# A transformer block with four-bit feed-forward weights: the last down pass staggered over four tiles, x rows in eight places, lookups queued behind the copies

## The chip, the cores and the metric

The kernel runs on one core of a Trainium2 chip. The metric is the device time of one execution in microseconds (us); lower is better. Kernels are compared by the median of several executions, and one execution of each is recorded by the hardware profiler. In a profile PE is TensorE (matmuls), PEld its weight loads, DVE VectorE, ACT ScalarE, POOL GpSimd, and SP the engine whose queue issues all DMAs here.

## The reference, cut to what matters

```python
x = x + layernorm(attention(layernorm(x)) @ Wo)          # 2048 rows of 1024
h = layernorm(x)
Wg, Wu, Wd = (NF4[codes] * scale_of_64 for each matrix)  # 2752 x 1024, 2752 x 1024, 1024 x 2752
inter = silu(h @ Wg.T) * (h @ Wu.T)                      # 2048 x 2752
x = x + layernorm(inter @ Wd.T)                          # 2048 x 1024
```

The attention is causal, with 16 heads of 64 and rotary positions. Each feed-forward weight is a code from 0 to 15, looked up in a table of 16 values and multiplied by a scale that is shared by 64 inputs. The change touches only the last line: the product with `Wd`, its layer norm and the residual sum.

## The kernel before

Matrix products are made with three matmuls: each operand is split into a high part and the rest, and high x high, high x rest and rest x high are summed in PSUM (`mm3`, lines 112 to 117). The split is one ACT copy and one DVE subtraction (`split`, L120 and L121).

The stages follow each other: layer norm and the q, k, v projections, attention, output projection with residual (up to about 1710 us in the profile), gate and up products with their lookups (to about 2640), and then the down product (to the end).

**The down product.** `inter` lies in DRAM as 22 tiles for each half of the rows, `ind[g][kt]`. The output is made in four passes, for column half `n` and row half `g` in the order (0,0), (0,1), (1,0), (1,1). A pass uses all eight PSUM banks, one for each of its eight row tiles of 128 rows; for each `kt` an `it` tile of 1 MB is loaded (L613, the last one in two halves by L616) and multiplied into all eight banks with the weights `wd[n, kt]`. At the end of each of the first three passes eight ACT copies (`keep`, L632) bring the banks into SBUF, so that the next pass can have the banks. Since the layer norm goes over a whole row, a row tile is complete when both column halves are there: `finish` is called for row tiles 0 to 7 after the pass (1,0), and for 8 to 15 in the pass (1,1), the last one, where the right half is read from its bank directly.

**The lookups.** `down_weights` makes the weights of one `kt` from the codes by `looked_up`: three loads of codes and scales (`cs`, L489 to L491), then seven ACT lines (L498) and ten DVE operations, which together stand for the table as a sum of minima and maxima of straight lines, and the split. `make` says how far the lookups are to be by each step: in the first pass one ahead of PE, in the second pass up to 16 of the second column half, and the last six with `issue_after` behind the second pass's copies on ACT. These are not orders of issue but program order: a scheduler fixes each engine's instruction order when the program is built, by program order and by its own estimate of when each operand and slot is ready. [...]

**Slots in SBUF.** Tiles with one tag share a fixed number of slots, and a new tile waits until a slot of its tag is given up. Seven `hd` slots hold the `it` tiles and the kept sums of the left column half (two while the second pass runs, four while the third does, two in the last pass once row tiles 0 to 7 are finished). `cs` tiles have the three `pw` slots, the lookups' results `mp` the four `f4` slots, the x rows that `finish` loads the two `pb` slots, and the results `y` go to `f4` slots.

**The last pass.** The tiles with `kt >= NIT - LAST`, that is the last six, are held: PE is to use them bank by bank, so that the first bank is complete early and its `finish` can run beside the matmuls of the others. With two `hd` slots taken by sums, five are left for six held tiles. The scheduler resolved this in its own way: the built order has five held tiles used for all eight banks, and then the sixth for all eight.

**`finish`** (L634 to L643) for one row tile: load the x row tile, BNStats over both halves (L126), mean and variance (L128, L130), the power -1/2 on POOL (L132), the bias (L134), and for each half an ACT addition of the bias (L641), a DVE multiply-add into `y` (L642) and a store (L643).

Of the kernel before, what the change touches and what calls it, by code (L numbers as in the profile page):

```python
# [10 lines left out]
F32 = mybir.dt.float32  # L11
# [4 lines left out]
ALU = mybir.AluOpType  # L16
# [5 lines left out]
E = 1024  # L22
D = 64
I = 2752
P = 128
# [3 lines left out]
NIT = 22  # L29
# [28 lines left out]
def block_kernel(ctx, tc, x, wq, wk, wv, wo, gu_codes, gu_scales, d_codes, d_scales, cos_sin, out):  # L58
    nc = tc.nc
    V, A, G, T = nc.vector, nc.scalar, nc.gpsimd, nc.tensor  # L60
    load = nc.sync.dma_start
# [12 lines left out]
    def slot(tag, shape, dtype, name):  # L74
        assert int(np.prod(shape[1:])) * 4 <= SLOTS[tag][1] * 1024, (tag, shape)
        return sb.tile(shape, dtype, tag=tag, name=name, bufs=SLOTS[tag][0])
# [6 lines left out]
    def any_bank():  # L83
        turn[0] += 1
        return bank(BANK_ORDER[turn[0] % 8])
# [37 lines left out]
    def ln_stats(row):  # L123
        st = small.tile([P, 2, 6], F32, tag="st", name="st")
        for i in range(2):
            V.bn_stats(st[:, i, :], row[i])  # L126
        mv = small.tile([P, 2], F32, tag="mv", name="mv")
        V.bn_aggr(mv, st.rearrange("p a b -> p (a b)"))  # L128
        ve = small.tile([P, 1], F32, tag="ve", name="ve")
        V.tensor_scalar(ve, mv[:, 1:2], EPS, None, ALU.add)  # L130
        rs = small.tile([P, 1], F32, tag="rs", name="rs")
        G.tensor_tensor(rs, ve, nhalf, ALU.pow)  # L132
        nb = small.tile([P, 1], F32, tag="nb", name="nb")
        V.tensor_scalar(nb, mv[:, 0:1], rs, -1.0, ALU.mult, ALU.mult)  # L134
        return mv[:, 0:1], rs, nb
# [449 lines left out]
        ["pa"] * 4 + ["w"] * 3 + ["pa"] + ["xc"] * 3,  # L585
        ["pa", "xc"] + ["pa"] * 4 + ["w"] * 3 + ["pa", "xc"],
    )
    LAST = 6
    SECOND = 16
    wd = {}  # L590

    def down_weights(n, kt):

        ns = slice(n * 512, (n + 1) * 512)
        if kt % 2 == 0:
            t = slot(WD_TAGS[n][kt // 2], [P, 2, 2, 512], FR, "wd")
            wd[n, kt], wd[n, kt + 1] = t[:, :, 0], t[:, :, 1]
        t = wd[n, kt]
        rows = P if kt < NIT - 1 else D
        b1 = min(2 * kt + 1, 42)  # L600
        m = looked_up(
            d_codes[kt * P : kt * P + rows, ns], d_scales[2 * kt : 2 * kt + 1, ns], d_scales[b1 : b1 + 1, ns], rows
        )
        if rows == P:
            split(t[:, 0], t[:, 1], m)
        else:
            A.copy(t[:, 0], m)
            V.tensor_tensor(t[D:, 0], m[D:], f32(t[D:, 0]), ALU.subtract)

    def load_inter(g, kt):  # L610
        t = slot("hd", [P, 2, 2, 512], FR, "it")
        if kt < NIT - 1:
            load(f32(t), ind[g][kt])  # L613
        else:
            for a in range(2):
                load(f32(t[a * D : (a + 1) * D]), ind[g][kt][:D])  # L616
        return t

    def down(o, it_, w, tt, first, last):

        i = it_[:, tt // 4, :, tt % 4 * P : (tt % 4 + 1) * P]
        if not last:
            mm3(o, i, w, first, False)
        else:
            T.matmul(o, lhsT=i[:, 0], rhs=w[:, 0], start=False, stop=False)
            T.matmul(o, lhsT=i[:, 1], rhs=w[:, 0], start=False, stop=True)

    def keep(t, o, n):

        if t % 4 == 0:  # L630
            kept.setdefault(n, []).append(slot(("hd", "xc")[n], [P, 4, 512], F32, "kept"))
        return A.copy(kept[n][t // 4][:, t % 4], o)  # L632

    def finish(t, left, right):  # L634

        xt = slot("pb", [P, E], F32, "xt")
        load(xt, x1d[t * P : (t + 1) * P, :])
        y = slot("f4", [P, E], F32, "y")
        _, rs, nb = ln_stats((left, right))
        for src, h in ((right, slice(512, E)), (left, slice(0, 512))):  # L640
            A.activation(xt[:, h], xt[:, h], AF.Identity, bias=nb)  # L641
            V.scalar_tensor_tensor(y[:, h], src, rs, xt[:, h], ALU.mult, ALU.add)  # L642
            load(out[t * P : (t + 1) * P, h], y[:, h])  # L643

    kept = {}
    left = [(n, kt) for n in range(2) for kt in range(NIT)]

    def make(upto):
        while left and 2 * NIT - len(left) < upto:
            down_weights(*left.pop(0))  # L650

    for n in range(2):
        for g in range(2):
            os = [any_bank() for _ in range(8)]
            final = n == 1 and g == 1
            its = []
            for kt in range(NIT):

                make(kt + 1 if (n, g) == (0, 0) else NIT + min(4 + kt, SECOND) if (n, g) == (0, 1) else 2 * NIT)
                it_ = load_inter(g, kt)  # L660
                if final and kt >= NIT - LAST:
                    its.append(it_)
                    continue
                for tt in range(8):
                    down(os[tt], it_, wd[n, kt], tt, kt == 0, kt == NIT - 1)
            for tt in range(8):
                t = 8 * g + tt
                for i, it_ in enumerate(its):
                    kt = NIT - LAST + i
                    down(os[tt], it_, wd[n, kt], tt, False, kt == NIT - 1)  # L670
                if final:
                    finish(t, kept[0][t // 4][:, t % 4], os[tt])
                else:
                    last = keep(t, os[tt], n)
            if (n, g) == (0, 1):
                with tc.issue_after(last.ins):
                    make(2 * NIT)
            if (n, g) == (1, 0):
                for t in range(8):
                    finish(t, *(kept[i][t // 4][:, t % 4] for i in range(2)))  # L680
# [49 lines left out]
```

## Time and profile before

| | us |
|---|---|
| Median of 3 runs | 3162.13 (3154.66 to 3164.9) |
| The profiled execution | 3162.79 |
| Its span | 3161.0 |
| PE busy | 3007.8, 95% of the span |
| DVE, ACT, POOL busy | 2161.6, 1827.9, 700.3 |
| First down pass, last matmul starts | 2758.37 |
| Second pass, first matmul starts | 2765.32 |
| Third pass, first matmul starts | 2885.67 |
| Last pass, first matmul starts | 3003.54 |
| Last matmul starts | 3127.32 |
| Granted TensorE clock, mean | 0.977 |

The span is the time from the first to the last instruction in the profile; the execution's own time is a little longer. A line of the timeline gives the start, the length of an instruction (of the merged group, where there are several), its engine, its line in the program, the operation with the tile that it writes and the tiles that it reads, and in brackets the idle time of its engine ahead of it with what is thought to have ended it. For SPq the length is only that of issuing; the transfer lands later. Matmul ends are modelled: a matmul of 128 x 512 is shown with 0.39 us, while in a full stream one starts each 0.227 us.

### The profile page before, as it was taken

How to read it: one execution, taken by the hardware profiler on the slowest of the kernel's cores; microseconds unless marked ns; L12 is line 12 of the kernel's file. 1: busy time of each engine (PE TensorE's matmuls, PEld its weight loads, DVE VectorE, ACT ScalarE, POOL GpSimd, SP SyncE). 2: the span in 40 equal slices, each digit the busy share in tenths (PEclk: the TensorE clock that was granted, in tenths of full speed). 3: DMA queues.
4: the chain of work that ended last, by engine and by line, in shares of the span. 5: the costliest groups of instructions: out<-in, count | busy, mean ns of one | idle time of the engine just before them, and what ended most of it. 6: DMA issues, size and time to landing. Idle time of an engine off the chain costs nothing.

```text
span 3161.0 us, 43388 instructions
## 1 busy us (share of the span) xinstructions
PE 3007.8 (95%) x14656; PEld 2474.5 (78%) x14656; DVE 2161.6 (68%) x4428; ACT 1827.9 (58%) x3846; POOL 700.3 (22%) x888
## 2 busy tenths in 40 slices
PE   7979999999999999989889999999999999999995
PEld 6868887787877777877667888888888888788884
DVE  7457778777877777776565986677666688974022
ACT  3246667666766666666555865556555567864011
POOL 4334444444443334453221000000000000000000
PEclk9989999999999999999989999999999999999997
DMA  8777666566637675643355332232222338685584
GB/s 311 251 233 228 206 207 198 169 187 189 201 133 198 194 223 158 218 141 111 113 193 167 120 114 94 100 106 95 94 93 94 107 101 289 212 283 193 193 328 145
DMA packets 246495, 552.31 MB, mean 175 GB/s; under 512 B 20224, under 2 KB 110336, under 8 KB 219136
## 3 DMA queue, kind: packets, MB, share of 16 engines
q1 hardware_dynamic: 246272, 549.53, 53.3%
q8 instruction: 116, 1.90, 0.2%
q14 instruction: 107, 0.88, 0.1%
HBM read 403.70 MB, written 145.75 MB: 174 GB/s over the span
## 4 chain that ended last, share of the span: by engine, by line
PE 79%; DMA 9%; DVE 6%; ACT 2%; issue 1%; SPq 1%; POOL 1%; DVEq 0%; ACTq 0%; POOLq 0%
PE bk L114 13%; PE bk L115 13%; PE bk L116 13%; PE pt L294 6%; PE qkv L114 5%; PE qkv L116 5%; PE qkv L115 5%; PE o L299 3%; PE s L255 3%; PE o L298 3%; PE s L257 3%; DMA wf<-in_wq 1%; DMA xc<-xd 1%; DMA cs<-in_d_codes 1%; PE pj L440 1%
## 5 line engine op out<-in xcount | busy, mean ns | idle before, releaser
L498 ACT ACTIVATE ln<-cs,bias 128x512 f32<-128x512 f32 x910 | 610.7, 717 | 133.6 <-DVE mp L505 37.1
L114 PE MATMUL bk<-x,wt 128*128 128x512 f32 x1376 | 535.8, 390 | 0.0
L115 PE MATMUL bk<-x,wt 128*128 128x512 f32 x1376 | 535.4, 389 | 0.0
L116 PE MATMUL bk<-x,wt 128*128 128x512 f32 x1376 | 535.2, 389 | 0.0
L284 POOL TENSOR_SCALAR prob<-prob,rc 128x512 f32<-128x512 f32 (+3 forms) x640 | 405.3, 654 | 407.8 <-DVE rc L279 241.1
L262 ACT ACTIVATE prob<-s,mxs 128x512 f32<-128x512 f32 (+3 forms) x640 | 400.8, 629 | 158.4 <-DVE mxs L261 144.0
L121 DVE TENSOR_TENSOR pw<-pt,pw 128x512 fp32r<-128x512 f32 (+3 forms) x640 | 376.8, 601 | 130.8 <-ACT pw L120 128.9
L261 DVE TENSOR_REDUCE mxs<-s 128x1 f32<-128x512 f32 (+3 forms) x640 | 379.5, 601 | 99.4 <-PE s L257 60.0
L120 ACT CAST pw<-pt 128x512 fp32r<-128x512 f32 (+3 forms) x640 | 323.1, 525 | 165.5 <-PE pt L294 135.1
L132 POOL TENSOR_TENSOR rs<-ve,nhalf 128x1 f32<-128x1 f32 x64 | 40.3, 643 | 1578.9 <-DVE ve L130 1553.8
L294 PE MATMUL pt<-ident,prob 128*128 128x128 f32 x2176 | 346.4, 276 | 3.2 <-DVE pw L121 3.0
L294 PEld LDWEIGHTS pt<-ident,prob 128*128 128x128 f32 x2176 | 267.5, 142 | 57.2 <-issue 4.4
L255 PE MATMUL s<-k,q 128*128 128x512 f32 (+3 forms) x640 | 268.1, 419 | 35.2 <-ACT prob L262 33.5
L114 PEld LDWEIGHTS bk<-x,wt 128*128 128x128 f32 x1376 | 258.8, 188 | 53.7
L115 PEld LDWEIGHTS bk<-x,wt 128*128 128x128 f32 x1376 | 258.6, 188 | 53.7
L116 PEld LDWEIGHTS bk<-x,wt 128*128 128x128 f32 x1376 | 258.5, 188 | 53.5
L114 PE MATMUL bk<-wd,it 128*128 128x512 f32 x672 | 262.6, 391 | 6.6 <-ACT kept L632 6.6
L115 PE MATMUL bk<-wd,it 128*128 128x512 f32 x672 | 262.4, 390 | 0.0
L116 PE MATMUL bk<-wd,it 128*128 128x512 f32 x672 | 261.8, 390 | 0.0
L299 PE MATMUL o<-pw,v 128*128 128x512 f32 (+3 forms) x640 | 250.9, 394 | 4.9 <-DVE pw L121 4.4
L298 PE MATMUL o<-pw,v 128*128 128x512 f32 (+3 forms) x640 | 247.7, 388 | 5.5 <-ACT pw L120 4.7
L114 PE MATMUL qkv<-xc,w 128*128 128x512 f32 x576 | 234.7, 407 | 14.5 <-ACT w L173 8.5
(124 smaller groups left out, 5516.3 us busy)
## 6 DMA issues: line engine op xcount, KB each, us to landing
xc<-xd SPq DMA_DIRECT2D x96, 1024.0 KB, 9.0
it<-ind SPq DMA_DIRECT2D x84, 1024.0 KB, 6.2
ind<-hl SPq DMA_DIRECT2D x84, 512.0 KB, 2.6
q<-qs SPq DMA_DIRECT2D x128, 256.0 KB, 6.9
cs<-in_gu_scales SPq DMA_DIRECT2D x172, 128.0 KB, 3.1
cs<-in_gu_codes SPq DMA_DIRECT2D x86, 256.0 KB, 2.9
tab<-in_cos_sin SPq DMA_DIRECT2D x32, 512.0 KB, 9.8
xd<-xr SPq DMA_DIRECT2D x16, 1024.0 KB, 6.6
```

The lines of the kernel that those rows point to most:

```text
L114: r = T.matmul(o, lhsT=w[:, 0], rhs=xx[:, 0], start=first, stop=False)
L115: T.matmul(o, lhsT=w[:, 0], rhs=xx[:, 1], start=False, stop=False)
L116: T.matmul(o, lhsT=w[:, 1], rhs=xx[:, 0], start=False, stop=last)
L121: V.tensor_tensor(lo, src, f32(hi), ALU.subtract)
L255: mm = T.matmul(s, lhsT=q[:, 0, j * P : (j + 1) * P], rhs=k[:, b:e], start=True, stop=False)
L261: V.tensor_reduce(mx, s, AX.X, ALU.max, negate=True)
L262: A.activation(prob[i][:, j, : e - b], s, AF.Exp, bias=mx, accum_out=sums[:, j % BATCH, i : i + 1])
L284: G.tensor_scalar(p, p, rc[:, jj % BATCH, i : i + 1], 0.0, ALU.mult, ALU.add)
L294: T.transpose(pt[:, j * P : (j + 1) * P], prob[kb // 4][:, j, kb % 4 * P : (kb % 4 + 1) * P], ident)
L298: T.matmul(o[:, cs], lhsT=v[:, kb, :], rhs=pw[:, 0, cs], start=kb == 0, stop=False)
L299: T.matmul(o[:, cs], lhsT=v[:, kb, :], rhs=pw[:, 1, cs], start=False, stop=kb == nk - 1)
L498: A.activation(ln, c8, AF.Identity, bias=bias_of[ab], scale=ab[0])
```

## The change

Three things change. The number of held tiles in the last pass, `LAST`, goes from six to four. `finish` loads its x row tile into one of eight slots by the number of its row tile (four `f4`, two `pb`, two `pw`) in place of the two `pb` slots, and writes its result over it, so that the tile `y` is gone. And in the second pass the lookups for the second column half are traced with `issue_after` behind the last copy of the first pass, which holds their ACT instructions behind that copy in ACT's order; the call that asked for everything in the later passes is dropped, since everything is asked for by then.

```diff
-    LAST = 6
+    LAST = 4
     SECOND = 16
+    XT_TAGS = ["f4"] * 4 + ["pb"] * 2 + ["pw"] * 2
     wd = {}
...
     def finish(t, left, right):
 
-        xt = slot("pb", [P, E], F32, "xt")
+        xt = slot(XT_TAGS[t % 8], [P, E], F32, "xt")
         load(xt, x1d[t * P : (t + 1) * P, :])
-        y = slot("f4", [P, E], F32, "y")
         _, rs, nb = ln_stats((left, right))
         for src, h in ((right, slice(512, E)), (left, slice(0, 512))):
             A.activation(xt[:, h], xt[:, h], AF.Identity, bias=nb)
-            V.scalar_tensor_tensor(y[:, h], src, rs, xt[:, h], ALU.mult, ALU.add)
-            load(out[t * P : (t + 1) * P, h], y[:, h])
+            V.scalar_tensor_tensor(xt[:, h], src, rs, xt[:, h], ALU.mult, ALU.add)
+            load(out[t * P : (t + 1) * P, h], xt[:, h])
 
     kept = {}
+    last = None
...
             for kt in range(NIT):
-
-                make(kt + 1 if (n, g) == (0, 0) else NIT + min(4 + kt, SECOND) if (n, g) == (0, 1) else 2 * NIT)
+                if (n, g) == (0, 0):
+                    make(kt + 1)
+                elif (n, g) == (0, 1):
+
+                    with tc.issue_after(last.ins):
+                        make(NIT + min(4 + kt, SECOND))
                 it_ = load_inter(g, kt)
```

## The prediction

> **What bounds the kernel now.** I read the page's busy shares first (PE 95%, so whatever shortens the run must take out PE idle time or the time after the last matmul), then the idle time of PE by stage, then the timeline around each gap. All that the change touches lies after 2640 us: the four down passes. The table by stage (columns: length, then busy us and instructions of PE, PEld, DVE, ACT, POOL, granted clock, DMA share, GB/s):
>
> ```profile
> 2640.00:2759.00 119.00, 118.75 (x524) 98.02 (x523) 109.82 (x197) 93.19 (x143) 0.00 (x0) 1.00 0.74 241
> 2759.00:2765.00 6.00, 0.00 (x0) 0.00 (x0) 6.00 (x11) 6.00 (x12) 0.00 (x0) 0.89 0.90 352
> 2765.00:2885.00 120.00, 119.69 (x518) 98.95 (x519) 62.78 (x109) 52.38 (x84) 0.00 (x0) 0.98 0.71 237
> 2885.00:3004.00 119.00, 119.00 (x527) 98.57 (x526) 39.75 (x72) 36.64 (x60) 0.00 (x1) 1.00 0.62 212
> 3004.00:3116.00 112.00, 112.00 (x495) 92.64 (x494) 20.12 (x49) 11.28 (x18) 4.75 (x8) 1.00 0.67 254
> 3116.00:3122.00 6.00, 2.03 (x9) 1.34 (x8) 0.00 (x0) 0.00 (x0) 0.00 (x0) 1.00 0.75 175
> 3122.00:3128.00 6.00, 5.34 (x16) 3.98 (x16) 4.20 (x11) 0.00 (x0) 0.55 (x1) 0.72 0.00 0
> 3128.00:3161.00 33.00, 0.00 (x0) 0.00 (x0) 16.69 (x43) 10.67 (x16) 3.83 (x7) 0.56 0.67 223
> ```
>
> See three holes in PE and nothing else: 2759 to 2765, 3118 to 3122, and the 33 us after the last matmul. The timeline at the first hole:
>
> ```profile
> 2757.49 0.59 SPq L491 DMA_DIRECT2D cs<-in_d_scales  x1
> 2758.20 3.31 SPq L613 DMA_DIRECT2D it<-ind  x5
> 2758.37 0.39 PE L626 MATMUL bk<-wd,it 128*128 128x512 f32 x1
> ...
> 2760.58 1.04 ACT L632 COPY kept<-bk 128x512 f32<-128x512 f32 x2
> ...
> 2765.32 0.77 PE L114 MATMUL bk<-wd,it 128*128 128x512 f32 x1 [6.56 <-ACT kept L632]
> ```
>
> The releaser named is ACT, but the first copy was done at about 2761.1. The first `it` load of the pass was issued at 2758.20, behind the lookups' `cs` loads in SP's queue; the DMA view puts loads of that moment at 7.0 us or more to landing, that is 2765.2. So two things made the hole: copies behind lookups on ACT, and, ending later, `it` loads behind `cs` loads on SP. The second hole, and the end:
>
> ```profile
> 3115.34 1.09 SPq L616 DMA_DIRECT2D it<-ind  x2
> 3122.37 0.77 PE L625 MATMUL bk<-wd,it 128*128 128x512 f32 x1 [4.34 <-DMA it<-ind]
> ...
> 3146.43 0.99 SPq L643 DMA_DIRECT2D out<-y  x2
> 3147.53 0.37 SPq L637 DMA_DIRECT2D xt<-x1d  x1
> 3148.73 1.33 ACT L641 ACTIVATE xt<-xt,nb 128x512 f32<-128x512 f32 x2 [2.49 <-DMA xt<-x1d]
> ...
> 3151.36 0.40 SPq L637 DMA_DIRECT2D xt<-x1d  x1
> 3152.34 1.33 ACT L641 ACTIVATE xt<-xt,nb 128x512 f32<-128x512 f32 x2 [2.28 <-DMA xt<-x1d]
> ```
>
> The sixth held tile has no `hd` slot until a held one is given up, so its load starts at 3115.34, and all eight banks end together at 3127.5. Then eight `finish` calls run with two `pb` slots for x rows: load, ACT, DVE, some 3.7 us a row, one after another.
>
> **What the Trainium skill says.** "TensorE: Matmul & The Clock Gate", the part on the HAM clock gate: an idle window of about 3.4 us throws PE to half clock, and it takes about as much sustained work to come back. The trace agrees: after 2765.32 and after 3122.37 the first dozen or so matmuls start 0.43 us apart instead of 0.227. So a hole costs more than its length. "DMA: Bandwidth & Descriptors", anatomy of one DMA: a semaphore wait is served on the issuing sequencer before dispatch. So on SP a waiting load holds all behind it, which the first hole shows. The same page, on bandwidth, names 435 GB/s as the ceiling on the fabric side; the trace runs at 425 GB/s with a DMA share of 1.03 in 3030 to 3040, so I take 430 as full.
>
> **The change, part by part.** Sums are against the profiled execution (span 3161.0, time 3162.79, that is 1.8 outside the span; 0.7 above the median of 3162.13). A pass is 22 x 8 x 3 - 8 = 520 matmuls x 0.2267 = 117.9 us (2885.67 to 3003.54 confirms it).
>
> 1. Lookups behind the first pass's copies. In the built order ACT now has the eight copies straight behind the last first-half lookup, and SP has the six first `it` loads of the second pass ahead of the `cs` load of lookup 3. Lookup 21's codes were read by 2724, so these loads leave as soon as PE frees slots, over 10 us before they are wanted. ACT is idle by then; the copies (0.5 us a bank) run as at 2882.70, where PE didn't wait. Removed: 2765.32 - 2758.60 = 6.7 us of hole, and the slow clock behind it: the second pass took 2885.67 - 2765.32 = 120.4 instead of 117.9, 2.5 us. Sum 9.2.
>  What it costs: the head start. Before, four lookups and most of a fifth of the second half were made in the first pass (ACT casts at 2731, 2738, 2744, 2750), and sixteen were done by 2837. Now they start at about 2760. The pace where nothing blocked is 6.3 us (2737.7, 2744.0, 2750.3); sixteen end at about 2861. The second pass's copies, which stand behind them on ACT, are due from 2873, the weights from 2876. Margin 12 us, hence 0. At the first pass's pace with loads in the way (eleven lookups from 2648.5 to 2724.2, 6.9 each) they end at 2870: still 0. On SP `it` 20 and 21 stand behind `cs` 15 (about 2842, wanted after 2867); the third pass's first `it` behind `cs` 18 (2861 to 2865, lands about 5 to 7 later, wanted at 2876). Bounds: 0 to +5. Lookups 16 to 21 stand behind the second pass's copies in both kernels.
>
> 2. x rows into eight places (`f4` x4, `pb` x2, `pw` x2), result over the row. No instruction is added: 16 loads, 32 ACT, 32 DVE, 32 stores as before. What moves is when loads go. Six x rows now stand among the third pass's `it` loads on SP, and the three in `pw` wait for the last lookups' `cs` slots (about 2914, 2920 and 2924 in the old times). Behind these stand `it` 7, 8, 9, which go at 2914.5, 2920.5, 2925; wanted at 2885.7 + 5.44k = 2923.8, 2929.2, 2934.7. With the least landing of 4.7 us, plus 1.2 for each half megabyte ahead, they land at 2920.4, 2926.4, 2931. Margin 3 us; I take 0, bounds 0 to +6 in all.
>  In the last pass the first eight `finish` calls, whose sixteen stores stand among the `it` loads on SP, end at about 21 us into the pass (DVE, 8 x (4 x 0.64 + 0.5) = 24 from 3001) instead of 44. DMA has 8.5 MB in this stretch, 20 us at 430 GB/s; `it` 7 then lands about 31 in, wanted at 38. Hidden; the cover is five `hd` slots of prefetch.
>
> 3. Four held tiles. Two `hd` slots hold the left sums, five are left: four held and the one before. They fit, so banks end one by one: 11 matmuls, 2.5 us apart. `it` 21 takes the slot that `it` 16 gives up 92.5 into the pass; with the 7.0 us that it took before it lands at 99.6. The built order puts 15 matmuls ahead of its first use: 98 + 3.4 = 101.4. So the second hole goes: 3122.37 - 3117.87 = 4.5, and 16 matmuls in 5.2 instead of 3.6: sum 6.1. Margin 1.8, bounds 0 to +4 with the clock.
>
> 4. The end. Before: 3161.0 - 3127.5 = 33.5 us after the last matmul. Now all x rows are in SBUF long before, and DVE works at 2.4 to 3.0 us a tile against PE's 2.5, so at the last matmul only two tiles or so are left. By the DVE order, from PE's end: BNStats of the last bank to 0.7; the product of tile 13 and small ones to 2.6; `pow` on POOL and `nb` back at 3.7; ACT of tiles 14 and 15 to 5.5 (each 0.7); last two products to 6.5; store 2.0 to 2.8 (min and median of the stores at the end). I take 9.3. Lower bound 7 (one tile alone), upper 14 (DVE a further tile and a half late). Removed: 24.2, bounds 19 to 26.
>
> Sum: 9.2 + 6.1 + 24.2 = 39.5. Span 3121.5, this execution 3123.3, on the median 3122.6: **3123**.
>
> **Rivals.**
> A. The transfers come late: x rows and `it` loads meet in the third pass, or the stores and loads at the start of the last. For it: margins of 2 to 7 us, and in 3020 to 3060 DMA is full. Against: PE didn't stall there with DMA at 1.03. Two or three waits of 3 to 5 us and a clock dip: 3127 to 3140, say 3133.
> B. DVE becomes the bound of the staggered end: its instructions wait in order for PE, POOL and ACT, so each tile costs 3.7 us as now. 8 x (3.7 - 2.5) = 9.6 later: 3133.
> C. The stagger doesn't come about (the last `it` is late again). Then only the x rows and the first hole help: tail of 8 x 3 = 24 instead of 33.5, and 9.2: 3144.
> D. Slower. With the head start gone, the second pass's copies on ACT stand behind sixteen lookups, and PE can't begin the third pass without banks. Late by 16p - 113 us at p us a lookup; this eats 39.5 from p = 9.5, and at p = 10 the time is 3172 or so with the clock. The worst seen is 6.9. For it: each `cs` load is now behind an `it` load that waits for PE. Against: PE frees a slot each 5.44 us, faster than lookups eat.
>
> **How the numbers follow.** Forecast 0.72, A 0.11, B 0.07, C 0.05, D 0.03, and 0.02 that gains and losses cancel. The forecast's own range: 3161.0 + 1.8 - (9.2 + 6.1 + 26) = 3121.5 at best, 3143 with all upper bounds at once (5 + 6 + 4 + 4.7), 3133 with half of them. The runs of before spread from 3154.7 to 3164.9, so I widen downwards by 7. To leave no more than 2 in 10 out: 3114 to 3136. What this kernel's measurement can tell from no change is 0.3%, 9.5 us: faster 0.94, same 0.02, slower 0.04.
>
> **What would show it.** PE without a gap over 1 us from 2640 to about 3112 and 1.00 clock throughout; the copies of the first pass at about 2755.5, without activations in between; last ACT cast of the sixteen before 2873; `it` 21 issued about 9 us before its first use; products spread over the last 20 us of PE, and 9 us from the last matmul to the end. A gap at the start of the third pass would be D, one in the middle of it or about 20 to 40 us into the last pass A, and over 14 us after the last matmul B. It would be wrong, too, if PE's clock fell where now it is 1.00.

## The result

| | before | changed |
|---|---|---|
| Median, us (4 runs each) | 3163.52 (3154.66 to 3175.01) | 3127.32 (3123.55 to 3129.2) |
| Ratio, 95% interval | | 0.9882 (0.9849 to 0.9916) |
| Span of the profiled execution | 3161.0 | 3125.7 |
| PE busy | 3007.8, 95% | 3003.9, 96% |
| Granted clock, mean | 0.977 | 0.982 |

The span is 35.3 us shorter. That number holds something that is not the change's work: up to the last matmul of the first down pass both programs do the same on PE, yet that matmul starts at 2761.06 us instead of 2758.37, 2.7 later. So from here on I measure from that matmul to the end of the span and call this stretch T. It was 3161.0 - 2758.37 = 402.6 before and 3125.7 - 2761.06 = 364.6 after: a gain of 38.0 us, where the prediction's sum was 39.5.

The profile after, by stage (the columns are those of the table of before):

```profile
2759.00:2765.00 6.00, 6.00 (x28) 4.96 (x27) 4.34 (x8) 6.00 (x12) 0.00 (x0) 1.00 0.83 291
2765.00:2879.00 114.00, 114.00 (x505) 94.33 (x503) 98.14 (x173) 84.34 (x130) 0.00 (x0) 1.00 0.75 244
2879.00:2885.00 6.00, 5.42 (x25) 4.26 (x24) 3.95 (x7) 5.74 (x11) 0.00 (x0) 1.00 0.78 314
2885.00:3100.00 215.00, 214.41 (x946) 177.11 (x945) 55.22 (x113) 41.62 (x65) 4.77 (x8) 1.00 0.73 262
3100.00:3117.00 17.00, 16.83 (x75) 13.60 (x73) 15.78 (x41) 7.81 (x12) 3.30 (x6) 1.00 0.36 134
3117.00:3126.00 9.00, 0.00 (x0) 0.00 (x0) 5.04 (x12) 2.79 (x5) 1.10 (x2) 0.74 0.58 216
```

PE's busy time equals the length of the stage in the first two rows. In the third and fourth 0.6 us each is missing, and the clock is 1.00 until the last matmul. The three holes of before are now two cracks and 9 us at the end. DVE, idle for most of the last pass before, works 15.78 of the 17 us ahead of PE's end.

The timeline at the first pass's end, where 6.7 us had been lost (the changed kernel has the `it` loads at L614 and L617 and the copies at L633):

```profile
2757.86 3.95 SPq L614 DMA_DIRECT2D it<-ind  x2
2758.32 4.01 ACT L633 COPY kept<-bk 128x512 f32<-128x512 f32 x8 [31.16 <-PE bk L627]
2761.06 0.39 PE L627 MATMUL bk<-wd,it 128*128 128x512 f32 x1
2761.29 0.39 PE L114 MATMUL bk<-wd,it 128*128 128x512 f32 x1
```

All eight copies are one block with no activation in between, ACT had waited 31 us for the banks, and PE goes from pass to pass in 0.23 us, its normal step. At the second pass's end:

```profile
2871.90 0.62 ACT L120 CAST wd<-mp 128x512 fp32r<-128x512 f32 x1 [3.05 <-DVE mp L511]
2871.93 0.33 SPq L489 DMA_DIRECT2D cs<-in_d_codes  x1
2873.51 6.16 SPq L614 DMA_DIRECT2D it<-ind  x3
2876.18 4.01 ACT L633 COPY kept<-bk 128x512 f32<-128x512 f32 x8 [3.66 <-PE bk L627]
2879.90 0.47 PE L114 MATMUL bk<-wd,it 128*128 128x512 f32 x1 [0.58 <-DMA it<-ind]
```

The sixteenth lookup's cast is done 3.7 us before the copies can start. But the DVE operation that releases this cast (L511) is also the one that gives up the `cs` slot for which SP's queue waits, and the third pass's first `it` load stands behind those `cs` loads: it goes at 2873.51 and PE gets it at 2879.90, 0.74 us after its normal step. And the end:

```profile
3116.44 0.39 PE L627 MATMUL bk<-wd,it 128*128 128x512 f32 x1
3116.87 0.70 DVE L126 BATCH_NORM_STATS2 st<-bk 128x6 f32<-128x512 f32 x1 [0.23 <-PE bk L627]
3119.17 2.56 ACT L641 ACTIVATE xt<-xt,nb 128x512 f32<-128x512 f32 x4 [1.94 <-DVE nb L134]
3122.03 0.74 DVE L642 SCALAR_TENSOR_TENSOR xt<-kept,rs,xt 128x512 f32<-128x512 f32 x1
```

The last product ends at 3122.77, 6.1 us after PE (which ends at 3116.44 + 0.23), and the last store 2.9 later.

### The profile page after: what moved, and what is told of

It reads as the page before. It is cut to its first block, busy times and chain, and to the rows that moved or that the text cites. A ratio compares the mean times of both kernels' runs of the same rounds, so it can differ in the third digit from the quotient of the medians.

```text
span 3125.7 us, 43392 instructions
## 1 busy us (share of the span) xinstructions
PE 3003.9 (96%) x14656; PEld 2470.5 (79%) x14656; DVE 2161.1 (69%) x4428; ACT 1831.5 (59%) x3846; POOL 702.8 (22%) x888
## 4 chain that ended last, share of the span: by engine, by line
PE 42%; DMA 3%; DVE 3%; ACT 1%; issue 1%; SPq 0%; DVEq 0%; POOLq 0%; POOL 0%; ACTq 0%
PE bk L114 13%; PE bk L116 13%; PE bk L115 13%; DMA cs<-in_d_codes 1%; DMA out<-xt 1%; PE pj L440 0%; PE pj L441 0%; PE pj L442 0%; DMA it<-ind 0%; DMA y<-yd 0%; DVE mp L511 0%; DMA cs<-in_d_scales 0%; PE pt L148 0%; DVE st L126 0%; DVE mp L504 0%
```

## The experiments

T and its parts, in us, for all executions that were profiled. "Gap 2" and "gap 3" stand ahead of the second and third pass, beyond a normal step of 0.227; "last pass" runs from its first to its last matmul start; "tail" is from there, less one step, to the end of the span. A pass of 520 matmuls without a gap takes 117.87 from start to next start, the last one 117.64.

| | gap 2 | gap 3 | last pass | tail | T | median |
|---|---|---|---|---|---|---|
| before | 6.72 | 0 | 123.78 | 33.45 | 402.6 | 3163.5 |
| changed | 0 | 0.74 | 118.59 | 9.03 | 364.6 | 3127.3 |
| `no_order` | 3.92 | 0 | 117.80 | 9.02 | 369.9 | 3130.2 |
| `before_pool_it` | 2.26 | 0 | 125.05 | 32.91 | 397.4 | 3160.0 |
| `late_copies` | 0 | 17.59 | 117.64 | 9.06 | 382.2 | 3130.0 |
| `no_xrows` | 0 | 0 | 117.96 | 17.67 | 371.8 | 3129.7 |
| `last6` | 0 | 1.26 | 124.64 | 18.85 | 381.1 | 3137.8 |
| `last5` | 0 | 0.16 | 117.64 | 8.09 | 362.2 | 3120.7 |
| `last3` | 0 | 1.85 | 117.64 | 11.72 | 367.5 | 3123.0 |
| `best` | 0 | 0 | 117.64 | 8.94 | 362.8 | 3122.5 |
| `best5` | 0 | 0 | 118.33 | 8.53 | 363.1 | 3121.5 |
| `after_again` | 0 | 2.00 | 117.64 | 9.09 | 366.7 | 3122.9 |

Medians of `late_copies`, `before_pool_it`, `last5` and `last3` are single runs; `no_order`, `no_xrows`, `last6`, `best` and `best5` have four, `after_again` six.

**The first hole with the order undone.** In `no_order` the lookups are again traced without the hold behind the copies.

```diff
-                if (n, g) == (0, 0):
-                    make(kt + 1)
-                elif (n, g) == (0, 1):
-
-                    with tc.issue_after(last.ins):
-                        make(NIT + min(4 + kt, SECOND))
+                make(kt + 1 if (n, g) == (0, 0) else NIT + min(4 + kt, SECOND) if (n, g) == (0, 1) else 2 * NIT)
```

> The changed kernel with the lookups of the second column half in their old place (no issue_after in the second pass); four held tiles and x rows in eight places stay. From the last matmul of the first pass to the end of the span the kernel before took 402.6 us and the changed one 364.6. Theory (the part's own worth is the first hole with its slow clock, 9.2, less the 0.7 that the third pass starts late in the changed kernel): 373, a hole of 6 to 7 us at the start of the second pass, none at the start of the third; 3135 or so in all. Rival (the hole was a chance of that one run, or is closed by the other two parts): 365, no hole over 1 us.

Measured: T 369.9, ratio to before 0.9912 (0.9884 to 0.994). The timeline of this kernel around the hole:

```profile
2754.95 0.59 SPq L491 DMA_DIRECT2D cs<-in_d_scales  x1
2755.65 3.20 SPq L614 DMA_DIRECT2D it<-ind  x5
2758.04 1.05 ACT L633 COPY kept<-bk 128x512 f32<-128x512 f32 x2
2758.11 0.39 PE L627 MATMUL bk<-wd,it 128*128 128x512 f32 x1
2762.26 0.76 PE L114 MATMUL bk<-wd,it 128*128 128x512 f32 x1 [3.76 <-ACT kept L633]
```

The hole is back, but with 3.9 us instead of 6.7. Here the `it` load left at 2755.65, 2.5 us before PE's last matmul of the pass; before it was 0.2 us ahead. In both, PE starts about 7 us after the issue (6.6 here, 7.1 before). I read from these two executions that the hole's size depends on when, within a lookup's period, the pass happens to end; two can't prove it. The expected T of 373 was too high by about as much as the hole came out small. The profile again names ACT as releaser, yet its first two copies were done at 2759.1, three us before PE moved.

**Which of two waits ended that hole.** `before_pool_it` is the kernel before with only the second pass's `it` loads issued from POOL's queue.

```diff
-    def load_inter(g, kt):
+    def load_inter(g, kt, load=load):
...
-                it_ = load_inter(g, kt)
+                it_ = load_inter(g, kt, G.dma_start if (n, g) == (0, 1) else load)
```

> The kernel before, with only the inter tiles of the second down pass loaded from POOL's queue in place of SP's; copies on ACT still stand among lookups, in the same order as before. The profile names ACT as the releaser of the first hole (6.7 us), though the first copy was done 2.7 us after the last matmul. Theory (the loads behind the lookups' loads on SP end last): the hole shrinks to the copies' part, 2 to 4 us. Rival (the copies behind lookups on ACT end last, as the profile's bracket says): the hole stays at 6 to 7 us or what is left from the last lines of lookups on ACT. The other holes and the end stay: 4.5 with slow clock, 33 after the last matmul.

Measured: a hole of 2.26 us, and this time the named releaser is right. Its timeline:

```profile
2741.60 0.77 POOL L613 DMA_DIRECT2D it<-ind  x1 [1038.84 <-PE bk L116]
2760.84 0.39 PE L626 MATMUL bk<-wd,it 128*128 128x512 f32 x1
2762.71 1.04 ACT L632 COPY kept<-bk 128x512 f32<-128x512 f32 x2
2763.33 0.50 PE L114 MATMUL bk<-wd,it 128*128 128x512 f32 x1 [2.10 <-ACT kept L632]
```

The first `it` load now leaves 19.5 us before it is wanted, and what is left is the copy, which waits on ACT for a lookup's activations and starts 1.9 us after the last matmul. So the hole of before had both causes, one over the other: SP's queue ended last and made it 6.7; with SP's part gone, ACT's alone makes 2.3. The change removes both at once: with the activations held, the `cs` loads too stand behind the pass's first `it` loads on SP.

**The rival that ends slower.** `late_copies` holds the second pass's copies behind the twentieth lookup of that pass, which is as if lookups were slower: this is rival D.

```diff
-    SECOND = 16
+    SECOND = 20
...
                     last = keep(t, os[tt], n)
+                    if (n, g) == (0, 1):
+                        after(last, made[1, SECOND - 1])
```

`made` keeps the ACT cast of each lookup's split.

> The changed kernel with 20 instead of 16 lookups of the second column half asked for in the second pass, and that pass's copies held behind the 20th on ACT: what the lost head start costs when it isn't covered. Theory (the copies wait for the lookups at 6.3 to 7.0 us each; the sixteenth ended 4 us ahead of them in the changed kernel): the third pass starts 21 to 24 us later, with 2.5 us of slow clock, 388 to 396 from the last matmul of the first pass to the end. Rival (the pace of the lookups is set by PE's slots, not by ACT and DVE, and they speed up when asked for early): less than 10 us later, under 375.

Measured: T 382.2, that is 17.5 over the changed kernel: gap 3 and its slow clock are 18.4 longer, the last pass 0.95 shorter. Timeline:

```profile
2875.68 0.62 ACT L120 CAST wd<-mp 128x512 fp32r<-128x512 f32 x1 [2.73 <-DVE mp L512]
2875.72 0.33 SPq L640 DMA_DIRECT2D xt<-x1d  x1
2876.16 1.32 SPq L616 DMA_DIRECT2D it<-ind  x3
2876.21 4.00 ACT L635 COPY kept<-bk 128x512 f32<-128x512 f32 x8
2881.74 0.76 PE L114 MATMUL bk<-wd,it 128*128 128x512 f32 x1 [17.43 <-DMA it<-ind]
```

Twenty lookups end 2875.68 - 2746.05 = 129.6 us after the first pass, 6.48 each. The prediction's formula, late by (lookups x pace) - 113, gives 20 x 6.48 - 113 = 16.6; the pass was 17.6 late. So rival D is real: late lookups do delay the third pass. That its price comes out is in part luck. The formula was made for the copies on ACT, and these freed the first bank at about 2876.8, which alone would have made PE 12.7 us late (its normal step was 2864.15). The other 4.9 are SP's: the `it` load left only when the twentieth lookup had ended, behind an x row, and reached PE 5.6 us after its issue. My expectation here was above the measurement; at the changed kernel's 6.93 us a lookup the formula gives 25.6. The whole time of this one execution, 3129.96 beside 3127.3, would hide the 17.5: the first pass of this execution ended 15 us earlier than that of the changed kernel.

**The end, one part at a time.** `no_xrows` keeps the order and the stagger of four and puts `xt` back into two `pb` slots with `y` in `f4`; `last6` keeps the order and the eight places and puts `LAST` back.

```diff
-        xt = slot(XT_TAGS[t % 8], [P, E], F32, "xt")
+        xt = slot("pb", [P, E], F32, "xt")
...
+        y = slot("f4", [P, E], F32, "y")
```

> The changed kernel with x rows back in the two pb slots and the result in a tile of its own; four held tiles and the order of lookups stay. From the last matmul of the first pass to the end: 364.6 in the changed kernel. Theory (two slots make a row tile cost 3.7 us in the staggered end too, as they did before): the eight row tiles end 8 x 3.7 after the first bank is complete, 18 us after the last matmul instead of 9: 373 to 374. Rival (the stagger alone hides the loads of the x rows, since a bank takes 2.5 us of PE): 9 to 11 us after the last matmul, 365 to 367.

```diff
-    LAST = 4
+    LAST = 6
```

> The changed kernel with six held tiles again; x rows in eight places and the order of lookups stay. From the last matmul of the first pass to the end: 364.6 in the changed kernel. Theory (six don't fit in five slots, the last tile comes late and all banks end together, DVE then needs about 2.7 us for each of eight row tiles): hole of 4 to 5 us with slow clock behind it, some 21 to 23 us after the last matmul: 382 to 384. Rival (the loads of the x rows were nearly all of the end, and with them gone the eight row tiles pass quickly): 5 for the hole and 12 to 14 after the last matmul: 373 to 375.

Ratios to before: 0.9906 (0.9887 to 0.9925) and 0.9929 (0.9914 to 0.9944). With the kernels before and after this makes a table of four tails: neither part 33.45, x rows alone 18.85, stagger alone 17.67, both 9.03. Each part alone is worth about 15 us, together 24.4, not 30; I put this down to tiles that are finished beside PE and no longer need a fast `finish` at the end. In `no_xrows` the x loads still limit the end (timeline):

```profile
3116.08 0.40 SPq L638 DMA_DIRECT2D xt<-x1d  x1
3119.90 1.33 ACT L642 ACTIVATE xt<-xt,nb 128x512 f32<-128x512 f32 x2 [2.59 <-DMA xt<-x1d]
3123.35 1.33 ACT L642 ACTIVATE xt<-xt,nb 128x512 f32<-128x512 f32 x2 [2.12 <-DMA xt<-x1d]
```

ACT takes a row tile in 3.45 us here and waits for `xt` between them, as before (3.61). In `last6` the eight tiles come as fast as DVE can make them. From the first statistics of these tiles to the last product it is busy 20.17 of 20.47 us, 2.6 us a tile (columns as in the table by stage):

```profile
3113.25:3133.72 20.47, 4.76 (x14) 3.40 (x13) 20.17 (x52) 10.24 (x16) 4.39 (x8) 0.58 0.47 173
```

It also brings back the second hole (timeline):

```profile
3105.43 1.09 SPq L617 DMA_DIRECT2D it<-ind  x2
3107.73 0.39 PE L116 MATMUL bk<-wd,it 128*128 128x512 f32 x1
3112.51 0.47 PE L626 MATMUL bk<-wd,it 128*128 128x512 f32 x1 [4.40 <-DMA it<-ind]
```

The last `it` load leaves 2.3 us before PE runs out of other work, and takes 7.1 to be usable. In the changed kernel it left at 3091.48 and was first used at 3100.12, 8.6 later, without a gap.

**How many held tiles.** Only the number differs, 5 or 3 instead of 4.

> The changed kernel with five held tiles in place of four. Five just fit in the five slots, and in the built order the last tile's first use comes 39 matmuls, 8.8 us, after the first use of the tile ahead of the held ones. Theory (slots decide, and a bank that takes 14 matmuls, 3.2 us, leaves DVE time enough): no hole, 7 to 8.5 us after the last matmul against 9.0; 363 to 365 from the last matmul of the first pass to the end, against 364.6. Rival (any number over four makes the last tile late): a hole of 3 us or more with slow clock: 368 or more.

> The changed kernel with three held tiles. A bank takes 8 matmuls, 1.8 us. Theory (DVE needs some 2.6 us for a row tile and falls behind): 13 to 15 us after the last matmul against 9.0. Rival (the end is a chain of one row tile, whatever the pace of the banks): 9 to 10.

Tails: 11.72 with three, 9.03 with four, 8.09 with five (one execution each for three and five). With five there is no second hole either. With three, a bank is complete each 1.8 us (8 matmuls), faster than DVE's 2.6 a tile, and DVE ends behind; it was less behind than I had expected. T of `last3` holds 1.85 us of gap 3 as well, at a place that the number doesn't touch.

**Code loads off SP's queue.** `best` issues the down lookups' `cs` loads from POOL's queue, and moves BNStats and what hangs on them earlier in the program order. `best5` has the first of the two and five held tiles.

```diff
-    def looked_up(codes, s0, s1, rows, tags=None):
+    def looked_up(codes, s0, s1, rows, tags=None, load=load):
...
-            ..., rows
+            ..., rows, load=G.dma_start
...
-        _, rs, nb = ln_stats((left, right))
+        _, rs, nb = early(ln_stats, (left, right))
```

The last pair of lines is in `best` alone.

> The changed kernel with the down lookups' loads on POOL's queue, so that they and the inter tiles no longer wait for each other on SP, and with the statistics of finish at a higher priority, so that the fourth instruction from the last bank no longer stands behind BNStats of the last bank on DVE. Theory (both waits found in the changed kernel are taken out): no gap at the start of the third pass (0.7 before), sixteen lookups done 8 us or more ahead of the copies instead of 4, 8 us after the last matmul instead of 9: 362 to 364 from the last matmul of the first pass to the end against 364.6. Rival (loads from POOL's queue cost more per load, and lookups get slower): the third pass starts 2 us late or more, 367 or more. In the whole time the gain is too small to tell from noise.

> The changed kernel with the down phase's lookups' code loads on POOL's queue and five held row tiles instead of four. From the last matmul start of the first pass to the end of the span: 361 to 363 us (changed kernel 364.6), with no gap ahead of the third pass, because SP's queue no longer holds code loads ahead of the third pass's activations, and 8 us after the last matmul (9.0 with four). If the fifth held tile's larger demand on VectorE's time early in the last pass or on the loads costs more than it saves, a stall shows within the last pass and the stretch stays at 364 or more. In the whole time some 2 to 3 us less than the changed kernel on the same chip, which is less than the spread of the earlier stages, so no verdict between the two is expected.

> The changed kernel once more, unaltered, on the chip of the run beside it. The stretch from the last matmul start of the first pass to the end of the span repeats 364 to 366 us, with the gap ahead of the third pass between 0 and 2 us (it hangs on when the sixteenth lookup's loads land), and 9 us after the last matmul. Whole time 3120 to 3130.

`best` has a ratio to before of 0.9889 (0.987 to 0.9908). `best5` and `after_again` ran on one chip, where before had 3156.91 (11 runs). Their medians, 3121.5 (3115.4 to 3125.2) and 3122.9 (3110.9 to 3130.8), can't be told apart. From the fixed point the two are 363.1 and 366.7, and it shows why. The changed kernel, once more:

```profile
2870.84 4.60 SPq L614 DMA_DIRECT2D it<-ind  x3
2876.94 0.47 PE L114 MATMUL bk<-wd,it 128*128 128x512 f32 x1 [1.84 <-DMA it<-ind]
2878.64 0.63 PE L114 MATMUL bk<-wd,it 128*128 128x512 f32 x1
2879.06 0.63 PE L115 MATMUL bk<-wd,it 128*128 128x512 f32 x1
```

Gap 3 is 2.0 us this time, and a stretch of slow matmuls (0.43 us apart, the last two lines) costs 1.73 more, so T lies 0.7 above what I expected. In `best5`:

```profile
2866.13 0.62 ACT L120 CAST wd<-mp 128x512 fp32r<-128x512 f32 x1 [2.73 <-DVE mp L511]
2868.07 9.39 SPq L614 DMA_DIRECT2D it<-ind  x3
2873.97 4.01 ACT L633 COPY kept<-bk 128x512 f32<-128x512 f32 x8 [7.22 <-PE bk L627]
```

The first `it` load of the third pass leaves 8.7 us before the last matmul start of the second at 2876.72, and there is no gap. ACT waits 7.2 us for the banks instead of 3.7. `best5` lost 0.7 us in the last pass, 0.55 of it in one wait at 3033.44, so its T came out just above the 361 to 363 expected. Neither `best` nor `best5` lost anything ahead of the third pass, and their T is 1.5 to 3.9 below that of the two executions of the changed kernel; whether this would show in a median, these runs can't tell.

Nor do they show that it takes POOL's queue. `no_xrows` differs from the changed kernel only in `finish`, and in the second pass its SP, ACT and DVE run the same instructions in the same order, code loads on SP included. Yet its sixteenth lookup came 106.2 us after the first pass, sooner than in `best5`, and the third pass's first load left 8.65 us ahead too (timeline; that pass's last matmul started at 2874.45):

```profile
2865.80 0.33 SPq L614 DMA_DIRECT2D it<-ind  x1
```

So six executions with the same second pass and the code loads on SP have a gap 3 of 0, 0.16, 0.74, 1.26, 1.85 and 2.00 us. In five of them the sixteenth lookup came after 110.5 us or more and the first load left 3.9 to 5.7 us ahead. What made the sixth quicker is open. The early statistics in `best` brought 0.1 in the tail, where 1 was expected: the last product ended 0.5 earlier and the last store took longer.

## Why the prediction was right, and where it was off

It said 3123 us (3114 to 3136) and faster; the runs gave 3127.3, and 3122.9 in the later set, where that is 34.0 below before (ratio 0.9889, 0.9867 to 0.9911). Since the earlier stages move by several us from one execution to the next, the test of the working is T: predicted 402.6 - 39.5 = 363.1, measured 364.6 and 366.7. By its steps:

1. **Lookups behind the copies.** Right in what it removes: both causes of the first hole existed, `it` behind `cs` ended last, and the named releaser was wrong (`before_pool_it`). The mis-sized term is the margin. Sixteen lookups were to end at 2861, 103 us after the first pass; the sixteenth's cast came at 2871.90, 111 after it, so 6.9 a lookup instead of 6.4. In the groups of DVE of the changed kernel, from 2762 to 2880 (columns: busy us, mean ns, then idle us and its releaser):

```profile
L511 DVE TENSOR_TENSOR mp<-mp,cs 128x512 f32<-128x512 f32 x16 | 11.0, 685 | 0.0
L493 DVE TENSOR_SCALAR l<-cs 128x512 f32<-128x512 int32 x16 | 6.8, 422 | 7.1 <-DMA cs<-in_d_codes 7.1
```

DVE waited 7.1 us for codes. These loads stand in SP's queue among `it` loads that wait for PE, which the prediction listed under rival D and priced at nothing. With the codes on POOL's queue (`best5`, the same groups and window) this wait is less, but not gone, and the sixteenth cast comes 107 us after the first pass:

```profile
L493 DVE TENSOR_SCALAR l<-cs 128x512 f32<-128x512 int32 x16 | 6.7, 420 | 3.9 <-DMA cs<-in_d_codes 3.9
```

ACT still came out early by 3.7 us, as the forecast had it; the step that failed is the sentence on SP, which let the third pass's first `it` go by 2865 and land with time to spare. It went at 2873.51, which is 2870.8 in the times of before. The slower pace was in the prediction, with an end at 2870, but it was tried on ACT's copies alone. Put into the sentence on SP it has that load go after 2870 and land 5 to 7 us later, at 2875 to 2877 or later with the `cs` loads ahead of it, where 2876 was wanted. The price was 0.8 us (0.74 and 0.08 of clock) in one execution and 3.7 (2.00 and 1.73) in the other, inside the bounds of 0 to +5 and not the 0 that I took. It is rival D's mechanism in small, by SP and not by ACT's copies. By the prediction's own signs the second execution even shows D: a gap over 1 us at the start of the third pass, and a clock that fell where it had been 1.00.

2. **x rows in eight places at no cost.** Right within 1 us. The third pass has no gap behind its first `it`. In the last pass the eight products on DVE ended 20 us in (21 predicted), but with the DMA share at 1.02 from 3015 to 3040 their last store was issued 30 us in, not 21. `it` 7, behind these stores on SP, left 31 us in, when the prediction had it landed, and reached PE 39 in. PE waited once, for it, 0.75 us at 3036.73, with 0.95 us lost in that pass in all; `after_again`, `last5` and `last3` lost nothing there, `best5` 0.7. Rival A in small.

3. **Four held tiles.** Right: the second hole is gone, and `last6` shows that the number and not the other parts removes it. The 6.1 us came in full; the margin of 1.8 held.

4. **The end.** 9.03 us against 9.3, with the predicted order of instructions: last BNStats done at 0.9 (0.7 predicted), `nb` at 3.5 (3.7), ACT at 5.1 (5.5), last product 6.1 (6.5), and 2.9 for the store instead of 2.8. Rival B, DVE as the bound at 3.7 us a tile, falls: without x loads to wait for, DVE needs 2.6 (`last6`). Rival C fell with step 3.

Sum of the misses: 0.8 + 0.95 - 0.3 = 1.45, against 364.6 - 363.1 = 1.5. What was left to chance is the 2.7 us upstream, and how large the first hole was in the one profiled execution of before: with its slow clock 9.2 us there, 6.9 in `no_order`.

On the slow clock the prediction used "TensorE: Matmul & The Clock Gate", the part on the HAM clock gate, for an idle window of about 3.4 us. The runs show that a hole need not be that long: after one of 2.00 us in `after_again` the clock fell to half, 1.2 us after PE had started again. The same part says that the window runs freely and that the number of slow matmuls varies from run to run, and with this the traces agree: 12 slow matmuls after the first hole of before, 14 after the shorter one of `no_order`, 8 in `after_again` (and 8 after the second hole of before, where the prediction read a dozen). Time lost after a hole, as the following pass's length over 117.87, and how long the granted clock was at half once PE had started again:

| hole, us | 0.74 | 1.85 | 2.00 | 2.26 | 3.92 | 6.72 | 17.59 |
|---|---|---|---|---|---|---|---|
| lost, us | 0.08 | 0.08 | 1.73 | 0.43 | 2.95 | 2.5 | 1.66 |
| at half clock, us | 0 | 0 | 3.41 | 0 | 6.00 | 5.14 | 3.26 |

(from the changed kernel, `last3`, `after_again`, `before_pool_it`, `no_order`, before, `late_copies`, in this order). The loss doesn't follow the hole's length. Where the clock fell, it is half of the time at half clock within 0.1 us; where it stayed at 1.00, the loss is a few slow steps. In before the half clock began at 2763.63, within the hole, and ended at 2770.46, 5.14 us after PE had started again:

```profile
2763.63:2770.46 6.83, 5.14 (x12) 4.11 (x13) 6.62 (x12) 6.61 (x12) 0.00 (x0) 0.50 1.01 420
```

To charge 2.5 us for the first hole's clock was right for this execution, but for another it is a number between 0 and 3.

## What to carry to other kernels

When two waits end at one instruction, look up the issue time of the load as well as the instruction that is named: the hole here had an ACT part of 2.3 us under an SP part of 6.7. With the loads moved alone, 2.3 were left (`before_pool_it`); where the copies came early by chance, the loads alone made 3.9 (`no_order`). Work that is moved off one hot moment keeps its loads in a queue: follow them to the next moment at which that queue matters, for there the margin is decided (here the load left 3.9 to 5.7 us ahead of the pass's last matmul in five executions, and 8.65 where nothing held it). And where two edits shorten the same tail, price them together: alone they brought 14.6 and 15.8 us, together 24.4.

## What the runs showed of the hardware that I had not expected

- Up to the end of the first down pass PE does the same work in all of these kernels, yet the last matmul of that pass started between 2746.05 and 2761.06 us over these twelve executions. A stage can gain or lose 17.5 us, as in `late_copies`, with the whole time hardly moved; only a fixed point inside the run shows it.
- A 1 MB load with a busy queue was usable 5.6 to 7.1 us after its issue in each timeline above where PE waited for it; at a DMA share of 1.02 (3015 to 3040 in the changed kernel) it took 11.1 to land in the median.
- A hole of 17.6 us cost less clock afterwards (1.66 us) than one of 3.9 (2.95), because less of the half clock was left when PE started again: 3.26 us against 6.00.
- The granted clock was at half in stretches of 3.41 us (`after_again`), 6.83 (before and `no_order`) and 17.07 (`late_copies`), that is one, two and five times 3.41.
